# Batch 0's second half of x on ScalarE's queue, and its first two weight sums in chunks

## The chip, the cores and the metric

The kernel runs on one core of a Trainium2 chip. The metric is the time of one execution on the device, in microseconds (us); a comparison is made from the median of several executions. All data are 32-bit floats.

## What is computed

The reference takes x of shape (8, 256, 1024), a bank of eight 1024 x 1024 adapters, a base weight with bias, a router and a low-rank mixture of experts:

```python
w = weight[adapter_ids]                        # one 1024 x 1024 adapter per batch element
y = einsum('bsi,boi->bso', x, w)               # the "cond" product
base_out = einsum('btd,od->bto', y, base_W) + base_b
probs = softmax(einsum('btd,nd->btn', y, router_W) + router_b)
w = top-8 of the 15 probabilities, each given to its expert by expert_map
h = einsum('btd,erd->bter', y, A)
lora = einsum('bter,eor->bto', h * w[..., None], Bm) * 2.0
out = x + base_out + lora
```

Only the first line pair matters here: for each of the eight batch elements, x[b] (256 x 1024) is multiplied by its own adapter, which is read from memory (4 MB for each batch element).

## The kernel before

The kernel has two stages. In the first, a loop over the eight batch elements makes y by a Strassen-Winograd product: the adapter and x are cut into 2 x 2 quarters (`a11`, `a12`, `a22`, `a21` of the adapter, `b11`, `b12`, `b21`, `b22` of x), and seven products of quarters take the place of eight. In the second stage the base weight is multiplied in the same way, over pairs of batch groups. The change touches only what happens for batch element 0, in the first 30 us of the first stage.

A quarter of the adapter is a tile `wt` of 128 partitions x 4 chunks x 512 elements (1 MB); for batch 0 it is loaded in two halves of two chunks, 512 KB each, by `load_w` (line 366). The halves are called a11h0, a11h1 and so on here. x of batch 0 comes in two halves too, 512 KB each, by `load_x0` (line 372): half 0 holds b11 and b21, half 1 holds b12 and b22. Half 0 is issued on ScalarE's queue as the first thing; half 1 is issued on SyncE's queue (SP), between the two halves of a12. So SP's queue holds, in this order: a11h0, a11h1, a12h0, x half 1, a12h1, a22h0, a22h1, a21h0, a21h1, and then the loads of batch 1.

TensorE multiplies in the order that the code writes it down: first 13 matrix products of an identity (`idle`, nothing is read from them), then for batch 0 the blocks

1. a11 . b11 into `pa`, a12 . b21 into `pb` (need x half 0 alone)
2. a22 . T4 into a second `pb` (needs x half 1, since T4 comes from all quarters of x)
3. S1 . T1 into `pc`, S2 . T2 into `pa`
4. S4 . b22 into `pc`, S3 . (b22 - b12) into `pa`

A block is four chunk products (line 297). [...]

VectorE makes the sums, also in the order of the code: `turns` makes T1, T2, T4 and b22 - b12 from x (lines 399 to 404, four instructions of 128 x 512), then `first_sum` S1 = a21 + a22 (line 412, for batch 0 in two halves, one for each half of a21), `second_sum` S2 = S1 - a11 (line 416, one instruction of 128 x 2048), `fourth_sum` S4 = a12 - S2 (line 424), `third_sum` S3 = a11 - a21 (line 420).

All engines but GpSimd follow the order of the code in this stage (a manual schedule). The `wt` tiles share eight buffers; a load of batch 1 can be issued when the buffer it gets is free, and SP waits at it.

Of the kernel before, what the change touches and what calls it, by code (L numbers as in the profile page):

```python
# [10 lines left out]
F32 = mybir.dt.float32  # L11
# [17 lines left out]
def kernel(  # L29
# [16 lines left out]
    nc = tc.nc  # L46
    P = 128
# [3 lines left out]
    KH = 4  # L51
    OH = 512
# [11 lines left out]
    wpool = ctx.enter_context(tc.tile_pool(name="w", bufs=8))  # L64
# [32 lines left out]
    late = const.tile([P, 4 * OH + 2 * KC * S // 2 + 512], F32, name="late")  # L97
# [4 lines left out]
    def place(*shape):  # L102
# [18 lines left out]
        for name, shape in dict(  # L121
            h=[NTT, ER], lg=[NTT, N], mx=[NTT], ex=[NTT, N], den=[NTT], rden=[NTT],
# [148 lines left out]
    with ExitStack() as phase:  # L271
# [84 lines left out]
        def load(b):  # L356

            x = xpool.tile([P, 2, 2, KH, P], F32, name="x")
            q = {}

            def load_w(name, i, halves=None):
                if name not in q:
                    q[name] = wpool.tile([P, KH, OH], F32, name="wt")
                t = q[name].rearrange("p (h k) o -> p h (k o)", h=2)
                for h in [slice(0, 2)] if halves is None else [ts(n, 1) for n in halves]:
                    nc.sync.dma_start(
                        t[:, h],
                        wq[ds(adapter, 1), i, h].rearrange("e h p f -> p (e h) f"),
                    )

            def load_x0(j, engine):
                engine.dma_start(x[:, j].rearrange("p i k t -> p (i k t)"), x0[j])

            if b == 0:

                load_x0(0, nc.scalar)
            else:
                nc.sync.dma_start(x.rearrange("p j i k t -> p (j i k t)"), xq[b - 1])
            adapter = nc.sync.value_load(
                ids_sb[0:1, b : b + 1], min_val=0, max_val=NA - 1  # L380
            )
            if b == 0:
                load_w("a11", 0, (0, 1))
                load_w("a12", 1, (0,))
                load_x0(1, nc.sync)
                load_w("a12", 1, (1,))
                load_w("a22", 3, (0, 1))
                load_w("a21", 2, (0, 1))
            else:

                for name, i in (("a22", 3), ("a21", 2), ("a11", 0), ("a12", 1)):
                    load_w(name, i)
            return x, q

        def turns(x):

            b11, b12, b21, b22 = x[:, 0, 0], x[:, 1, 0], x[:, 0, 1], x[:, 1, 1]
            t1 = tpool.tile([P, KH * P], F32, name="tt").rearrange("p (k t) -> p k t", k=KH)
            nc.vector.tensor_sub(t1, b12, b11)
            t2 = tpool.tile([P, KH * P], F32, name="tt").rearrange("p (k t) -> p k t", k=KH)  # L400
            nc.vector.tensor_sub(t2, b22, t1)
            t4 = tpool.tile([P, KH * P], F32, name="tt").rearrange("p (k t) -> p k t", k=KH)
            nc.vector.tensor_sub(t4, b21, t2)
            nc.vector.tensor_sub(b12, b22, b12)
            return t1, t2, t4

        def first_sum(q):
            q["s1"] = wpool.tile([P, KH, OH], F32, name="wt")
            parts = 2 if q is first else 1
            for n in range(parts):  # L410
                h = ts(n, KH // parts)
                nc.vector.tensor_add(q["s1"][:, h], q["a21"][:, h], q["a22"][:, h])  # L412

        def second_sum(q):
            q["s2"] = wpool.tile([P, KH, OH], F32, name="wt")
            nc.vector.tensor_sub(q["s2"], q["s1"], q["a11"])

        def third_sum(q):

            nc.vector.tensor_sub(q["a21"], q["a11"], q["a21"])  # L420

        def fourth_sum(q):
            q["s4"] = wpool.tile([P, KH, OH], F32, name="wt")
            nc.vector.tensor_sub(q["s4"], q["a12"], q["s2"])

        phase.enter_context(
            tc.manual_schedule(engines={EN.PE, EN.DVE, EN.Activation, EN.SP})
        )
        x, q = load(0)
        first = q  # L430

        idle = ps.tile([P, OH], F32, name="pb")
        for _ in range(13):
            nc.tensor.matmul(idle[:, :P], lhsT=ident, rhs=ident, start=True, stop=True)
        t1, t2, t4 = turns(x)
        first_sum(q)
        second_sum(q)
        fourth_sum(q)
        third_sum(q)
        waiting = None  # L440
        behind = deque()
        for b in range(B):
# [3 lines left out]
            if not last:  # L446
                x, nq = load(b + 1)
# [51 lines left out]
            if b == 0:  # L499
                by_s4()  # L500
                by_s3()
                nc.vector.tensor_add(m1[:, 0], pa, m1[:, 0])
                flip(m1[:, 0], m1[:, 0])
                first_sum(nq)
                second_sum(nq)
                fourth_sum(nq)
            elif not last:
                first_sum(nq)
                by_s4()
                if b == 1:  # L510

                    by_s3()
                    second_sum(nq)
                else:
                    second_sum(nq)
                    by_s3()
# [24 lines left out]
            if not last:  # L541
                q, t1, t2, t4 = nq, nt1, nt2, nt4
# [470 lines left out]
```

## Time and profile before

| what | value |
|---|---|
| median of 3 runs | 429.84 us (429.76 to 430.26) |
| the profiled execution, its own time | 430.95 us |
| span of the profiled execution | 429.2 us |
| TensorE matrix products | 423.7 us busy, 99% of the span |
| VectorE | 338.0 us, 79% |
| ScalarE | 163.7 us, 38% |
| bytes moved by DMA | 93.15 MB, 217 GB/s on average |
| issue of x half 1 on SP | 0.43 us, from issue to landing 7.5 us |
| one S1 half (128 x 1024), S2, S4, S3 (128 x 2048) on VectorE | 1226, 2292, 2292, 2283 ns |

The span is the time from the first to the last instruction of the profiled execution; its own time is 1.75 us longer. In the profile PE is TensorE's matrix product, PEld its weight load, DVE is VectorE, ACT is ScalarE, SPq and ACTq are the instructions by which SP and ScalarE issue transfers. A row of the timeline gives the start, the busy time, the engine and line, output and input tiles, how many instructions were merged, and in brackets how long the engine had been idle and what released it.

### The profile page before, as it was taken

The numbers are of one execution on the slowest core, as the hardware profiler recorded it, in microseconds if no ns is written. First come the engines' busy times: TensorE is split into PE (matmuls) and PEld (weight loads), VectorE is DVE, ScalarE is ACT, GpSimd is POOL, SyncE is SP. The second block draws the span as 40 slices with busy tenths as digits, with TensorE's granted clock in tenths as the row PEclk, the third lists the DMA queues.
The fourth block names the chain that finished last, engine by engine and source line by source line (L and its number), as shares of the span: only waits on it lengthen the run. The fifth ranks groups of instructions, "written<-read, shape, count | busy, mean of one in ns | idle before, by whom it ended". The sixth has DMA issues, their size and how long they took to land.

```text
span 429.2 us, 4059 instructions
## 1 busy us (share of the span) xinstructions
PE 423.7 (99%) x1246; PEld 218.0 (51%) x1246; DVE 338.0 (79%) x520; ACT 163.7 (38%) x442; POOL 35.3 (8%) x57
## 2 busy tenths in 40 slices
PE   8999999999999999999999999999999999999997
PEld 5444464644645546446446565445454454544444
DVE  0699999986887898898995668889983499848783
ACT  1119367965667658666826722300000000211000
POOL 0000000000000000000003401203321050000000
PEclk9999999999999999999999999999999999999999
DMA  7997987869677789592595250027182201715935
GB/s 245 417 361 281 324 337 289 281 246 359 198 274 244 290 314 348 213 356 93 184 413 187 98 220 1 2 65 302 43 326 98 73 0 47 272 49 168 348 122 195
DMA packets 26408, 93.15 MB, mean 217 GB/s; under 512 B 2322, under 2 KB 6290, under 8 KB 24082
## 3 DMA queue, kind: packets, MB, share of 16 engines
q1 hardware_dynamic: 26242, 92.36, 58.7%
q10 hardware_dynamic: 144, 0.52, 0.3%
q8 instruction: 10, 0.16, 0.2%
q14 instruction: 12, 0.10, 0.1%
HBM read 71.65 MB, written 21.23 MB: 216 GB/s over the span
## 4 chain that ended last, share of the span: by engine, by line
PE 91%; DVE 4%; DMA 4%; SPq 1%; issue 0%; DVEq 0%
PE pa L297 24%; PE pa L581 20%; PE pc L297 13%; PE pc L581 10%; PE pb L297 7%; PE ph L135 6%; PE pb L684 4%; PE pc L590 2%; DMA wt<-in_wq_dram 2%; DMA out_dram<-q 1%; PE pa L590 1%; DVE q L794 1%; PE pb L688 1%; DVE late L793 1%; PE pa L135 1%; DVE q L783 1%
## 5 line engine op out<-in xcount | busy, mean ns | idle before, releaser
L315 ACT COPY y<-late 32x256 f32<-32x256 f32 x256 | 103.0, 402 | 42.0 <-DVE late L250 39.1
L581 PE MATMUL pa<-wt 128*128 128x512 f32 x168 | 76.2, 593 | 0.1
L297 PE MATMUL pa<-wt,x 128*128 128x512 f32 x128 | 57.6, 593 | 0.4 <-DMA wt<-in_wq_dram 0.4
L297 PE MATMUL pa<-wt,tt 128*128 128x512 f32 x120 | 54.0, 593 | 0.0
L581 PEld LDWEIGHTS pa<-wt 128*128 128x128 f32 x168 | 31.8, 190 | 35.7 <-issue 32.8
L636 ACT COPY q<-pa 128x512 f32<-128x512 f32 x6 | 3.5, 586 | 106.1 <-PE pa L581 91.3
L297 PEld LDWEIGHTS pa<-wt,x 128*128 128x128 f32 x128 | 24.2, 190 | 30.9 <-issue 29.7
L261 ACT COPY hwT<-late 32x64 f32<-32x64 f32 x128 | 31.1, 243 | 16.1 <-DVE late L250 14.6
L297 PEld LDWEIGHTS pa<-wt,tt 128*128 128x128 f32 x120 | 22.3, 190 | 26.2 <-issue 25.9
L135 PEld LDWEIGHTS ph<-late,y 128*128 128x128 f32 x224 | 28.4, 189 | 3.3 <-issue 3.3
L297 PE MATMUL pb<-wt,x 128*128 128x512 f32 x64 | 29.1, 595 | 0.6 <-DMA wt<-in_wq_dram 0.6
L297 PE MATMUL pc<-wt,x 128*128 128x512 f32 x64 | 28.9, 594 | 0.0
L297 PE MATMUL pc<-wt,tt 128*128 128x512 f32 x64 | 28.8, 592 | 0.0
L135 PE MATMUL ph<-late,y 128*128 128x143 f32 x224 | 28.6, 284 | 0.0
L581 PE MATMUL pa<-y,wt 128*128 128x512 f32 (+1 forms) x64 | 26.4, 552 | 0.0
L581 PE MATMUL pc<-y,wt 128*128 128x512 f32 x56 | 26.3, 592 | 0.0
L581 PE MATMUL pc<-wt 128*128 128x512 f32 x56 | 25.8, 592 | 0.0
L412 DVE TENSOR_TENSOR wt<-wt 128x2048 f32<-128x2048 f32 (+1 forms) x9 | 18.4, 2046 | 7.9 <-PE pa L297 5.5
L667 POOL TENSOR_TENSOR wt<-wt 128x128 f32<-128x128 f32 x6 | 3.1, 512 | 261.3 <-DVE spare L341 219.5
L250 DVE STREAM_TRANSPOSE late<-late 128x512 f32<-128x512 f32 (+1 forms) x33 | 21.4, 647 | 1.1
L297 PEld LDWEIGHTS pb<-wt,x 128*128 128x128 f32 x64 | 12.0, 190 | 16.6 <-issue 14.3
L297 PEld LDWEIGHTS pc<-wt,x 128*128 128x128 f32 x64 | 12.1, 190 | 15.5 <-issue 14.8
(131 smaller groups left out, 537.7 us busy)
## 6 DMA issues: line engine op xcount, KB each, us to landing
wt<-in_wq_dram SPq DMA_DIRECT2D x28, 1024.0 KB, 5.5
x<-in_xq_dram SPq DMA_DIRECT2D x7, 1024.0 KB, 7.0
wt<-left_raw SPq DMA_DIRECT2D x7, 1024.0 KB, 7.6
xt<-in_xr_dram SPq DMA_DIRECT2D x12, 512.0 KB, 5.6
wt<-left_sum SPq DMA_DIRECT2D x7, 768.0 KB, 8.9
wt<-in_wq_dram SPq DMA_DIRECT2D x8, 512.0 KB, 8.2
spare<-in_bq_dram SPq DMA_DIRECT2D x4, 1024.0 KB, 5.2
left_raw<-spare SPq DMA_DIRECT2D x4, 1024.0 KB, 6.3
```

Of the source, the lines that this page charges most:

```text
L135: nc.tensor.matmul(ph[:, j, : ER + N], lhsT=y[:, k // KH, k % KH // 2, th, k % 2, bi, ts(j, P)], rhs=ar_sb[:, k, :], start=(j == order[0] ...
L250: nc.vector.transpose(half, of)
L261: lambda a=a, r=r: nc.scalar.copy(to[32 * r : 32 * r + 32, :, a, :], hw[32 * a : 32 * a + 32, :, ts(r, 32)],)
L297: nc.tensor.matmul(acc, lhsT=right[:, k, :], rhs=left[:, k, :], start=(first and k == 0), stop=(k == KH - 1), skip_group_check=True,)
L315: lambda a=a, r=r: nc.scalar.copy(y[32 * r : 32 * r + 32, :, :, a, :], m[32 * a : 32 * a + 32, :, :, r, :])
L412: nc.vector.tensor_add(q["s1"][:, h], q["a21"][:, h], q["a22"][:, h])
L581: nc.tensor.matmul(acc, lhsT=left[:, 2 * k + mi, :], rhs=right[:, k, at], start=(first and k == 0), stop=(up is None and k == 1), skip_gro ...
L590: nc.tensor.matmul(acc, lhsT=up[:, ts(mi, P)], rhs=hw[:, at], start=False, stop=True, skip_group_check=True,)
L684: nc.tensor.matmul(acc, lhsT=d, rhs=e, start=first, stop=not joins, skip_group_check=True)
L688: nc.tensor.matmul(acc, lhsT=ups[n], rhs=hw[:, 0, h], start=False, stop=True, skip_group_check=True,)
L783: add(q, q, xs[oh, th, i, j])
L793: soon.append(lambda: add(v[:, i, j], v[:, i, j], q))
```

## The change

Three things are done, all for batch 0. First, x half 1 moves from SP's queue to ScalarE's. ScalarE first copies one column of a11's first half into a corner of `late`, so that the transfer is issued only once a11h0 has landed. Second, the two halves of a12 are then loaded one after the other on SP. Third, S1 and S2 are made chunk by chunk and in turns: S1 of chunks 0 and 1, S2 of chunks 0 and 1, S1 of chunks 2 and 3, S2 of chunks 2 and 3, in place of S1 in two halves and S2 whole. Later batch elements make S1 and S2 as they did.

```diff
             if b == 0:
                 load_w("a11", 0, (0, 1))
-                load_w("a12", 1, (0,))
-                load_x0(1, nc.sync)
-                load_w("a12", 1, (1,))
+
+                nc.scalar.copy(late[:, :1], q["a11"][:, 0, :1])
+                load_x0(1, nc.scalar)
+                load_w("a12", 1, (0, 1))
                 load_w("a22", 3, (0, 1))
                 load_w("a21", 2, (0, 1))
...
         def first_sum(q):
             q["s1"] = wpool.tile([P, KH, OH], F32, name="wt")
-            parts = 2 if q is first else 1
-            for n in range(parts):
-                h = ts(n, KH // parts)
-                nc.vector.tensor_add(q["s1"][:, h], q["a21"][:, h], q["a22"][:, h])
+            nc.vector.tensor_add(q["s1"], q["a21"], q["a22"])
...
+        def first_sums(q):
+
+            for name in ("s1", "s2"):
+                q[name] = wpool.tile([P, KH, OH], F32, name="wt")
+            for h in range(2):
+                for k in (2 * h, 2 * h + 1):
+                    nc.vector.tensor_add(q["s1"][:, k], q["a21"][:, k], q["a22"][:, k])
+                for k in (2 * h, 2 * h + 1):
+                    nc.vector.tensor_sub(q["s2"][:, k], q["s1"][:, k], q["a11"][:, k])
...
         x, q = load(0)
-        first = q
...
         t1, t2, t4 = turns(x)
-        first_sum(q)
-        second_sum(q)
+        first_sums(q)
         fourth_sum(q)
         third_sum(q)
```

## The prediction

> **What bounds the kernel now.** I read the page first, then the waits of TensorE, then the timeline and the windows of the first 30 us.
>
> ```profile
> span 429.2 us, 4059 instructions
> PE 423.7 (99%) x1246; PEld 218.0 (51%) x1246; DVE 338.0 (79%) x520; ACT 163.7 (38%) x442; POOL 35.3 (8%) x57
> PEclk9999999999999999999999999999999999999999
> ```
>
> TensorE is busy all but 5.5 us, at full granted clock. The waits of TensorE's products after 26 us are an empty list, and those before 30 us are these:
>
> ```profile
> PE pb L434 <- POOL ident masks.py:199: 1.4, 1, 1.4
> PE pb L297 <- DMA wt<-in_wq_dram: 0.6, 1, 0.6
> PE pa L297 <- DMA wt<-in_wq_dram: 0.4, 1, 0.4
> ```
>
> So a time saved or lost before TensorE's S4 block (25.65 us) moves the end by as much, and nothing later can give it back. How much there is to win stands in TensorE's own timeline:
>
> ```profile
> 6.44 1.88 PE L297 MATMUL pa<-wt,x 128*128 128x512 f32 x4
> 8.76 1.98 PE L297 MATMUL pa<-wt,x 128*128 128x512 f32 x4 [0.44 <-DMA wt<-in_wq_dram]
> 10.72 1.98 PE L297 MATMUL pb<-wt,x 128*128 128x512 f32 x4
> 13.29 1.98 PE L297 MATMUL pb<-wt,x 128*128 128x512 f32 x4 [0.59 <-DMA wt<-in_wq_dram]
> 15.12 3.60 PE L297 MATMUL pb<-wt,tt 128*128 128x512 f32 x8
> 18.55 3.60 PE L297 MATMUL pc<-wt,tt 128*128 128x512 f32 x8
> 22.14 3.67 PE L297 MATMUL pa<-wt,tt 128*128 128x512 f32 x8
> 25.65 3.60 PE L297 MATMUL pc<-wt,x 128*128 128x512 f32 x8
> 29.08 1.45 PE L297 MATMUL pa<-wt,x 128*128 128x512 f32 x3
> ```
>
> Eight rows back to back take 3.43 us (25.65 to 29.08), one row 0.429. From 6.44 to 25.65 are 40 rows, 17.15 us, in 19.21: 2.06 us are lost. Of these 1.71 go before 13.29, waiting for a11h1, a12h0 and a12h1 in turn, 0.12 for restarting at 13.29 (1.83 us for four rows), and 0.24 around S2 (3.59 and 3.51 where 3.43 would do).
>
> The transfers are what is waited for. In half-microsecond windows (last two columns: DMA share, GB/s):
>
> ```profile
> 6.50:7.00 0.50, 0.50 (x3) 0.26 (x3) 0.00 (x0) 0.00 (x0) 0.00 (x0) 1.00 0.62 238
> 7.00:7.50 0.50, 0.50 (x3) 0.25 (x2) 0.00 (x0) 0.00 (x0) 0.00 (x0) 1.00 2.12 164
> 7.50:8.00 0.50, 0.50 (x2) 0.00 (x0) 0.00 (x0) 0.00 (x0) 0.00 (x0) 1.00 0.35 139
> 8.00:8.50 0.50, 0.32 (x1) 0.00 (x0) 0.00 (x0) 0.00 (x0) 0.00 (x0) 1.00 0.50 205
> 12.00:12.50 0.50, 0.50 (x2) 0.00 (x0) 0.44 (x1) 0.00 (x0) 0.00 (x0) 1.00 0.98 401
> ```
>
> From 9 us on the engines move some 418 GB/s without a pause, so a half of 512 KB takes 1.25 us; between 6.5 and 8.5 they stall, with packets in flight (a share of 2.12) but few bytes. In the packet records a dozen engines sit for 0.5 to 1.6 us on one 4 KB packet that began at 7.06 to 7.33, as a12h0 begins. The last of the 16 engines' reports of each transfer, also in the trace, gives the landings: a11h0 6.17, a11h1 8.72, a12h0 10.67, x half 1 11.96, a12h1 13.25, a22h0 14.53, a22h1 15.80, a21h0 17.09, a21h1 18.35.
>
> **The change, part by part.**
>
> *x half 1 leaves SP's queue.* SP saves one issue (0.43 us, plus about 0.2 of steps between). That is worth nothing by itself: a12h1 was issued at 5.06 us and landed at 13.25, so the queue's backlog, not SP, sets the landings. The issues of a22h0 to a21h1 come 0.6 us earlier in the same backlog.
>
> *ScalarE waits for a11h0, copies, issues.* a11h0 is there at 6.17; the copy of one column is some 0.24 us by the nearest row (32x64 copies, 243 ns), the issue 0.38 (x half 0's row). Behind the wait on ScalarE stands only the copy of `pa` at 10.78, four us later: hidden, and if that cover went, m0's copy delays nothing before the add at 26.44. First bytes come about 1.1 us after the start of an issue (x half 0: issue 0.74, first packet 1.86), so at 7.5 us.
>
> *What the second queue does to the landings.* [...] The trace has no stretch with both queues busy. [...] By the row of the stall, instead, x half 1 could fill the idle half of 7.5 to 8.5 us: 279 and 213 GB/s missing, 246 KB, and everything later lands 0.59 us earlier. [...]
>
> [...] T4 becomes the bound only if x lands after 12.9.
>
> *S1 and S2 by chunks.* Removed: two instructions of 1226 ns and one of 2292. Added: eight of 128 x 512. In `turns` a chunk of this size lasts 0.69 us, and starts follow 0.61 apart where an instruction doesn't need the one before it (13.52 to 14.13), 0.73 where it does. Each S2 chunk needs the S1 chunk two places earlier, so 0.61 holds: the eight end 7 x 0.61 + 0.69 = 4.96 us after the first begins, against 21.99 - 17.11 = 4.88 before. [...]
>
> What TensorE gains: S2's first chunks are ready at about 19.6, long before 22.1, so the 0.24 goes. [...]
>
> *Buffers.* SP's order of waits shows one shift: batch 1's a12 gets another buffer, that of batch 0's a11, and waits for S3 (ends at about 26.6) where it had been issued at 24.9. Queued behind it are the load of `spare` and the constants, 1.7 us later. Cover: batch 1's a12 is first used at 35.9, the constants at 42.2, landing before that at about 35.7. No cost.
>
> **Sum.** Middle landing: 15.12, 18.55, 21.98, 25.41, so -0.24 us. Late landing: 15.35, 18.78, 22.21, 25.64, so -0.01. With the chunk rule's price +0.1 to +0.3 of that back. I take -0.15: the profiled execution's 430.95 becomes 430.8. The profiled time is 1.1 us above the median of the runs; the difference carries over, 429.84 - 0.15 = 429.7 us.
>
> **Rivals.**
>
> *The second queue fills the stall.* For it: the engines are idle, not short of work, from 7.5 to 8.5. Against it: the sitting packets may block the whole engine. Worth: a12h0 at 11.3, a12h1 at 12.7, a21h0 at 16.5, so a22 . T4 begins at 14.9 and S4 at 25.2: -0.5; if the stall from 7.0 on also eases, 373 KB or 0.89 us, -0.75; if a12's first packets no longer stall, up to -1.3. Near 429.0.
>
> *The second queue adds a stall (slower).* The first packets of several transfers sit for long: about 0.6 us for x half 1 itself on four engines, 1.3 us and more for a12h0 on a dozen. If x's first packets, now amid a12h0's, sit 1.3 us and hold up SP's packets too, all later landings move by 1.3: a12h0 at 13.0, a22 . T4 at 16.6, a21h0 at 18.4, S4 at 26.9: +1.2, 431.0. It decides from about 0.8 us of added stall on. Against it: bytes and addresses are the same.
>
> *It doesn't do what it says.* If x half 1 gets its place only behind SP's backlog, the order is much as before: between -0.24 and 0, as T4 has 0.9 us of slack.
>
> **How the numbers follow.** About 0.2% (0.86 us) is what a measurement of this kernel can tell from no change. The likeliest case has 0.52, of which 0.49 lie within 0.86 us, 0.02 faster and 0.01 slower; its own range is 429.4 to 430.1. Filling the stall has 0.24: 0.19 over the bound, 0.05 within. The added stall has 0.21: 0.20 over, 0.01 within. The last rival has 0.03, within. Sums: faster 0.21, same 0.58, slower 0.21. The range 428.8 to 430.9 leaves out 1 in 10 at each end.
>
> **What would show it.** Right: a12h0 lands later than 10.67 and x half 1 by 12; a21h0 near 17.1; S1's third chunk at about 20.2; no wait before S2; S4's first product between 25.4 and 25.65. Wrong: a21h0 off 17.1 by more than 0.6 us, x half 1 after 12.9, or a wait of TensorE after 26 us.

## The result and the profile after

The changed kernel takes 432.32 us in the median of 6 runs (431.47 to 433.63). The kernel before, run beside it, takes 430.02 (429.76 to 430.26, 6 runs). The ratio is 1.0054, with a 95% interval of 1.0042 to 1.0066: slower by 2.3 us. The forecast was no measurable change at 429.7 us, with a range up to 430.9; the result lies outside it.

The six runs fall into two groups by the granted clock (the share of TensorE's full clock that the records show as granted). Three have 1.0 over the whole span and take 431.47, 431.55 and 431.73 us. Three have 0.995 to 0.996 and take 432.91 to 433.63. All six runs of the kernel before have 0.999 or 1.0. So there are two losses to explain: some 1.5 us in every run, and another 1.6 us in some of them. The profiled execution is the one of 431.55 us. From its page:

```profile
span 429.8 us, 4065 instructions
PE 422.4 (98%) x1246; PEld 218.0 (51%) x1246; DVE 337.4 (78%) x525; ACT 163.9 (38%) x443; POOL 36.3 (8%) x57
```

TensorE is busy for 1.3 us less than before, and the span is longer by 0.6: the difference is idle time. The waits of TensorE's products name it in one line:

```profile
PE pb L297 <- DVE tt L404: 2.8, 1, 2.8
```

The waits of before for a11h1 and a12h1 (0.4 and 0.6 us) are gone. One wait of 2.8 us for T4 (`tt`, made at line 404 of this kernel) has taken their place. TensorE's timeline shows where it lies:

```profile
6.29 3.67 PE L297 MATMUL pa<-wt,x 128*128 128x512 f32 x8 [0.17 <-DMA wt<-in_wq_dram]
9.98 3.70 PE L297 MATMUL pb<-wt,x 128*128 128x512 f32 x8
16.45 3.67 PE L297 MATMUL pb<-wt,tt 128*128 128x512 f32 x8 [2.77 <-DVE tt L404]
19.96 3.60 PE L297 MATMUL pc<-wt,tt 128*128 128x512 f32 x8
23.39 3.60 PE L297 MATMUL pa<-wt,tt 128*128 128x512 f32 x8
26.83 3.60 PE L297 MATMUL pc<-wt,x 128*128 128x512 f32 x8
```

The blocks of a11 and a12 now run without a gap, and end some 1.5 us earlier than before. Then TensorE stands for 2.77 us, and a22 . T4 begins at 16.45 instead of 15.12. S4 begins at 26.83, 1.18 us later than before. ScalarE's and VectorE's timelines show both ends of the cause:

```profile
6.18 0.19 ACT L385 COPY late<-wt 128x1 f32<-128x1 f32 x1 [3.75 <-DMA wt<-in_wq_dram]
6.19 0.34 ACTq L372 DMA_DIRECT2D x<-in_x_dram  x1
```

```profile
14.21 0.69 DVE L400 TENSOR_TENSOR tt<-x 128x512 f32<-128x512 f32 x1 [14.21 <-DMA wt<-in_wq_dram]
14.94 0.69 DVE L402 TENSOR_TENSOR tt<-x,tt 128x512 f32<-128x512 f32 x1
15.66 0.69 DVE L404 TENSOR_TENSOR tt<-x,tt 128x512 f32<-128x512 f32 x1
```

The gate opened and the transfer was issued at 6.19 us, as forecast. But VectorE's first sum of x starts at 14.21, 2.15 us later than before. (The releaser printed, a transfer of `wt`, is the one that happened to come last; the sum reads x alone, and x half 1's last report is at 14.11.) The packet records of the transfers put numbers on it: first packet, and the last of the 16 reports.

| transfer | before, landed | after, landed |
|---|---|---|
| a12h0 | 10.67 | 9.94 |
| x half 1 | 11.96 | 14.11 (issued 6.19, first packet 9.95) |
| a12h1 | 13.25 | 11.23 |
| a22h0 | 14.53 | 13.48 |
| a21h0 | 17.09 | 16.36 |

x half 1's first packet moved 3.76 us after its issue, when a12h0 was already there. So a12h0 shared the engines with nothing, and x half 1 overlapped the end of a12h1 and then a22h0. Between 11.0 and 12.5 us it got about half (331 of the 620 KB in the packet records); over its whole 3.71 us (9.95 to 13.66) its 512 KB are 141 GB/s, a third of the 418 that the engines move together.

After S4's first product everything is as it was. From there to the last row of TensorE's timeline the changed kernel takes 399.55 us (26.83 to 426.38), and so do six of the profiles of the experiments below, within 0.01. The first profile of before takes 400.13 (25.65 to 425.78): 0.15 of the excess is a wait at batch 1's S4, and 0.43 is a stall at 412 us. These 0.58 are why the two profiled times differ by 0.60 (430.95 and 431.55) where S4 differs by 1.18. From that last row to the run's own time it is 5.17 us in both. So the profiles show 1.03 us of the 1.5 between the medians: S4's 1.18 less the 0.15. The rest goes with the profiled executions of before, which stand above their median (see "The kernel before again"); why they do stays open.

### The profile page after: what moved, and what is told of

It is laid out like the page before. It is cut to its first block, busy times and chain, and to the rows that moved or that the text cites. A ratio compares the mean times of both kernels' runs of the same rounds, so it can differ in the third digit from the quotient of the medians.

```text
span 429.8 us, 4065 instructions
## 1 busy us (share of the span) xinstructions
PE 422.4 (98%) x1246; PEld 218.0 (51%) x1246; DVE 337.4 (78%) x525; ACT 163.9 (38%) x443; POOL 36.3 (8%) x57
## 4 chain that ended last, share of the span: by engine, by line
PE 95%; DMA 2%; SPq 1%; DVE 1%; issue 0%
PE pa L297 24%; PE pa L587 23%; PE pc L297 13%; PE pc L587 11%; PE pb L297 6%; PE ph L135 6%; PE pb L690 4%; PE pc L596 3%; DMA wt<-in_wq_dram 2%; PE pa L596 2%; PE pb L694 1%; PE pa L135 1%; PE pb L587 1%; SPq L366 1%; PE pb L596 0%; DMA ids_sb<-in_ids_dram 0%
## 5 line engine op out<-in xcount | busy, mean ns | idle before, releaser
L410 DVE TENSOR_TENSOR wt<-wt 128x2048 f32<-128x2048 f32 x7 | 16.0, 2281 | 5.5 <-PE pa L297 5.5
L297 PEld LDWEIGHTS pc<-wt,tt 128*128 128x128 f32 x64 | 12.2, 190 | 15.3 <-issue 14.8
```

The source lines that it names most:

```text
L297: nc.tensor.matmul(acc, lhsT=right[:, k, :], rhs=left[:, k, :], start=(first and k == 0), stop=(k == KH - 1), skip_group_check=True,)
L410: nc.vector.tensor_add(q["s1"], q["a21"], q["a22"])
```

## The experiments

The theory from this profile was: what costs the time is that x half 1's packets start late, and they start late because of what is in SP's queue when it is issued. Its rivals were a fixed delay of some 3.5 us on ScalarE's second transfer, the changed order of a12 and x by itself, and the chunked sums.

### The chunked sums alone

The loads of before, with S1 and S2 in chunks:

```diff
-        first_sum(q)
-        second_sum(q)
+        first_sums(q)
```

> The kernel before with S1 and S2 of batch 0 made chunk by chunk, x half 1 left where it was on SP's queue. Theory (the loss of the change comes from the queue alone, the chunks remove the S2 wait): S4's first product at 25.4 us in place of 25.65, time 0.2 us under the kernel before (429.8). Rival (the eight small sums cost: S1's third chunk comes late): a wait of 0.3 us or more within S1 x T1, time equal to or 0.1 to 0.3 us over before.

Measured: 430.04 us (13 runs) against 430.02, ratio 1.0000 (0.9992 to 1.0009). The chunks are not what made the kernel slower. The gain expected of them is not there either. TensorE's timeline and the waits of its weight loads say why:

```profile
17.44 3.71 PE L297 MATMUL pc<-wt,tt 128*128 128x512 f32 x8
20.99 3.60 PE L297 MATMUL pa<-wt,tt 128*128 128x512 f32 x8
24.42 3.60 PE L297 MATMUL pc<-wt,x 128*128 128x512 f32 x8
48.75 1.45 PE L297 MATMUL pa<-wt,x 128*128 128x512 f32 x3
```

```profile
PEld pc L297 <- DVE wt L421: 1.2, 3, 0.7
PEld pc L297 <- ACT late L499: 0.9, 1, 0.9
```

S2 follows S1 directly, and S4 follows S2 after 3.43 us, so the loss around S2 is gone. But S1 . T1 takes 3.55 us, since S1's third chunk is late (the first line of the waits, 0.7 at most). Of 0.24 us half is left, and the second line takes that back at batch 1's S4. From S4's first product to batch 1's S3 it is 24.33 us (24.42 to 48.75), where the changed kernel, without this wait, takes 24.03.

### The same chunks, all of S1 first

```diff
-            for h in range(2):
-                for k in (2 * h, 2 * h + 1):
+            for k in range(KH):
                     nc.vector.tensor_add(q["s1"][:, k], q["a21"][:, k], q["a22"][:, k])
-                for k in (2 * h, 2 * h + 1):
+            for k in range(KH):
                     nc.vector.tensor_sub(q["s2"][:, k], q["s1"][:, k], q["a11"][:, k])
```

> The kernel before with S1 in four chunks and then S2 in four chunks (all of S1 first, not in turns). Theory (with the chunks in turns the gain at S2 is lost again at S1's third chunk, which stood behind two S2 chunks): no wait of TensorE in S1 x T1 other than for a21h1, none before S2; S4's first product 0.3 to 0.6 us before that of the chunks in turns for like landings, time 0.2 to 0.5 us under the kernel before. Rival (the landings set the end, whatever the order of the sums): no difference over 0.15 us.

Measured: 430.33 (13 runs) against 430.20, ratio 1.0002 (0.9993 to 1.0010). In its profile S1 . T1 has no gap (18.07 to 21.50, 3.43 us) and S4 begins at 24.93, 0.5 later than with the chunks in turns, since a21h0 landed 0.63 later (16.62 and 15.99). But batch 1's S4 then waits 1.1 us for `late` (ScalarE's copy of `pc`), and from S4 to batch 1's S3 it is 24.57 us. The earlier S4 was handed back a batch later, as in the kernel with the chunks alone.

### The gate on x half 0

The transfer is issued at 4.16 us instead of 6.19:

```diff
-                nc.scalar.copy(late[:, :1], q["a11"][:, 0, :1])
+                nc.scalar.copy(late[:, :1], x[:, 0, 0, 0, :1])
```

> The changed kernel, but ScalarE's copy waits for x half 0 (lands at about 4.0 us) in place of a11h0 (6.17), so that x half 1 is issued at about 4.1 us, when SP has issued three transfers and not seven. Theory (a transfer of the second queue starts only behind what SP had issued long before: the delay is backlog): the first packet of x half 1 comes 1 to 2 us after its issue, at 5 to 6 us, not 3.7 us after it; it lands by 10, T4 is no bound, TensorE's wait of 2.8 us is gone, S4's first product at 25.0 to 25.6 us, time 429.4 to 430.0. Rival (an issue behind a wait on ScalarE always takes some 3.7 us to its first packet, or the second queue is served last): first packet at 7.8 us or after, landing at about 11.5 to 12; TensorE's wait shrinks to under 0.5 us as well, but the first packet tells the two apart.

Measured: 430.50 (13 runs) against 430.02, ratio 1.0012 (1.0004 to 1.0020); most of the loss is gone. The first packet came at 7.51, which is 3.35 us after the issue: nearly as late after it as in the changed kernel (3.76), so the 5 to 6 us expected were missed, and this run alone fits a fixed delay as well. Here x half 1 does share with a12, and the forecast's late landing happened almost to the digit (a12h0 at 11.73; the late case supposes 11.75, an estimate between 10.67 and 11.96, where a12h0 and x half 1 landed before, so in part by luck):

```profile
11.78 3.70 PE L297 MATMUL pb<-wt,x 128*128 128x512 f32 x8 [0.99 <-DMA wt<-in_wq_dram]
15.31 3.60 PE L297 MATMUL pb<-wt,tt 128*128 128x512 f32 x8
18.75 3.60 PE L297 MATMUL pc<-wt,tt 128*128 128x512 f32 x8
22.18 3.60 PE L297 MATMUL pa<-wt,tt 128*128 128x512 f32 x8
25.61 3.60 PE L297 MATMUL pc<-wt,x 128*128 128x512 f32 x8
```

The prediction's late landing has 15.35, 18.78, 22.21 and 25.64 for first bytes at 7.5 us: a12's block from 11.8 on (11.78 here), then 3.43 us for its eight rows and 0.12 for restarting. With that input its late case was right; it was the input that was wrong.

### SP held before a22

To shorten what is queued, SP waits until a11h0 is there (it stores 4 bytes of it to a scratch in memory) before it issues a22:

```diff
                 load_w("a12", 1, (0, 1))
+                nc.sync.dma_start(hold, q["a11"][:1, 0, :1])
                 load_w("a22", 3, (0, 1))
```

> The changed kernel, but SP waits for a11h0 (by a 4-byte store of one of its elements to a scratch in memory) before it issues a22h0, so that SP has four transfers issued when x half 1 is issued at 6.2 us, and not seven. The gate of x half 1 is unchanged. Theory (backlog): first packet of x half 1 at 7.3 to 8.5 us in place of 9.9, landing by 11.5 to 12.3, TensorE's wait for T4 under 0.5 us, S4's first product at 25.2 to 25.8, time 429.6 to 430.3. Rival (an issue behind a wait on ScalarE takes 3.7 us by itself): first packet still at 9.9, landing at 12.5 or after, wait for T4 over 1 us, time 431 or more.

Measured: 431.44 (6 runs) against 430.02, ratio 1.0037 (1.0023 to 1.0051). First packet at 9.60, 3.33 us after the issue at 6.27; x half 1 there at 13.88. The expectation of 7.3 to 8.5 was missed. (Two of the six runs, 432.89 and 433.12 us, have a clock of 0.995 and 0.996. The second of them is the profiled one; the clock is taken up below, and all the times here lie before it drops, at 16.71.) Leaving a22 and a21 out of the queue changes little; if the queue is the cause, it is what stands directly ahead: a11h1, then under way, and a12h0.

### SP held before a12

The same store one line earlier, so that only a11h1 is left in SP's queue when x half 1 is issued:

```diff
+                nc.sync.dma_start(hold, q["a11"][:1, 0, :1])
                 load_w("a12", 1, (0, 1))
```

> The changed kernel, but SP waits for a11h0 already before a12h0 (by a 4-byte store of one of its elements to a scratch in memory), so that when ScalarE issues x half 1 at 6.2 us only a11h1 is under way in SP's queue. Theory A (a transfer of the second queue waits for what stands in the DMA engines at its issue: in three profiles its first packet came as the transfer in progress and the next one had ended): first packet at 7.2 to 7.9 us, 1.0 to 1.6 after the issue; x half 1 and a12h0 share the engines and land at 9.5 to 11; no wait for T4; time 429.8 to 430.8. Theory B (an issue on ScalarE behind a wait takes 3.3 to 3.9 us to its first packet whatever the queue holds): first packet at 9.5 to 10, landing at 11.5 or later.

This is the run that decides. From ScalarE's, SP's, VectorE's and TensorE's timelines:

```profile
6.17 0.34 ACTq L374 DMA_DIRECT2D x<-in_x_dram  x1
```

```profile
6.63 3.55 SPq L368 DMA_DIRECT2D wt<-in_wq_dram  x6
```

```profile
9.97 0.69 DVE L403 TENSOR_TENSOR tt<-x 128x512 f32<-128x512 f32 x1 [9.97 <-DMA x<-in_x_dram]
```

```profile
11.18 3.70 PE L299 MATMUL pb<-wt,x 128*128 128x512 f32 x8 [1.24 <-DMA wt<-in_wq_dram]
14.72 3.60 PE L299 MATMUL pb<-wt,tt 128*128 128x512 f32 x8
```

Issued at the same time as in the changed kernel, the first packet came at 7.15, after 0.98 us, and x half 1 was there at 9.87 instead of 14.11. The fixed delay falls. Measured: 430.66 (18 runs) against 430.20, ratio 1.0013 (1.0006 to 1.0020). Now a12h0 is the one that is late (11.14), and TensorE waits 1.24 us for it; that is the price of holding the main queue, and the 2.3 us are not there.

The packet records of this run answer one more rival, that ScalarE's queue is served only after SP's. a12h0 was issued on SP at 6.63 us, 0.46 after x half 1, while a11h1 was under way. Its first packet moved at 8.91, 2.28 us after the issue, as x half 1's packets ran out (the last ended at 9.51; SP's store of 4 bytes stood ahead of it too). From 7.2 to 8.9 only ScalarE's queue moved bytes. So the delay belongs to neither queue: here it is SP's transfer that starts behind ScalarE's, where the expectation had the two sharing.

The first packets on ScalarE's queue, side by side:

| kernel | issue | first packet | later by | ahead in SP's queue |
|---|---|---|---|---|
| x half 0 (changed kernel) | 0.74 | 1.77 | 1.03 | nothing |
| SP held before a12 | 6.17 | 7.15 | 0.98 | a11h1 |
| gate on x half 0 | 4.16 | 7.51 | 3.35 | a11h0, a11h1 and more |
| SP held before a22 | 6.27 | 9.60 | 3.33 | a11h1, a12 |
| changed kernel | 6.19 | 9.95 | 3.76 | a11h1, a12, a22, a21 |

In each of the last three rows the packets begin as the second of SP's transfers ends: a11h1 (7.21 to 8.37 across the engines) in the first of them, a12h0 (8.67 to 10.23) in the second. In the second profile of the changed kernel and in the one with half of the fill (both below) it is 0.4 and 0.6 us after a12h0's last report. So in these runs a transfer on one queue started behind the one that was under way and the next that was issued before it, 512 KB each. Whether these are held in the DMA engines or in what hands transfers to them isn't settled by these runs.

### x half 1 on SP, last

The order of a12 and x alone, without a second queue (the chunked sums stay):

```diff
-                nc.scalar.copy(late[:, :1], q["a11"][:, 0, :1])
-                load_x0(1, nc.scalar)
                 load_w("a12", 1, (0, 1))
+                load_x0(1, nc.sync)
```

> The changed kernel with x half 1 issued on SP's queue directly behind a12h1, and no copy on ScalarE: the new order of landings without the second queue. Theory (the loss is x half 1 landing late at 14.1, of which the place behind a12 is a part and the start of the second queue 3.7 us after its issue is the rest): it lands at 12.2 to 13.3, T4 ends 2.3 later, TensorE waits 0.5 to 1.8 us for it, S4's first product at 25.2 to 26.2 us, time 430.2 to 431.3, between before and after, with few or no runs at a lower mean clock. Rival (the order alone costs nothing, it is the second queue): time within 0.3 of before.

Measured: 430.18 (12 runs) against 430.20, ratio 1.0001 (0.9992 to 1.0009). In TensorE's timeline:

```profile
15.26 3.67 PE L297 MATMUL pb<-wt,tt 128*128 128x512 f32 x8 [1.14 <-DVE tt L402]
25.64 3.60 PE L297 MATMUL pc<-wt,x 128*128 128x512 f32 x8
```

x half 1 lands at 12.92, which is the 12.9 from which the prediction let T4 become the bound, and the block begins 0.14 later than before. The expectation, that the order is part of the loss, was missed, and its rival holds: the order alone costs nothing. The loss is the rest, 12.92 to 14.11.

### Filling TensorE's wait

So the late landing of x half 1 is the cause of the part that every run has. For the other part, the clock, TensorE's wait is filled with products of the identity from which nothing is read, first 12, then 6:

```diff
                 pd = ps.tile([P, OH], F32, name="pb")
+                for _ in range(12):
+                    nc.tensor.matmul(pd[:, :P], lhsT=ident, rhs=ident, start=True, stop=True)
                 block(pd, q["a22"], t4, True)
```

> The changed kernel with 12 products of the identity (128 columns, nothing is read from them) ahead of a22 x T4, which fill TensorE's wait of 2.8 us for T4. Theory (the runs of the changed kernel at 433 us, with a mean clock of 0.995, lose some 1.5 us since the clock gate lowers the clock for a window after the idle time): all runs at clock 1.0 and at 431.4 to 431.7, median 431.5. Rival (the spread comes from the transfers): the runs spread from 431.5 to 433.6 as before, median over 432.

Measured: 431.90 (5 runs) against 430.02, ratio 1.0044 (1.0031 to 1.0057), all at a clock of 0.999 or 1.0. The fill was too long: in the profiled execution, the slowest (432.63), it ended only at 17.6 us and delayed the block itself. So it doesn't separate the clock's cost from its own. The changed kernel was run again for more executions, and with half of the fill:

> The changed kernel once more, beside the next one. Theory (the clock gate drops the clock for one window of 3.4 us when the wait for T4 falls within one of its windows): the runs stand in two groups, about 431.6 at mean clock 0.999 to 1.0 and about 433 at 0.995 to 0.996, a third to two thirds of them in the second. Rival (the second group was chance in the first six runs): one group, all at clock 1.0.

> The changed kernel with 6 products of the identity (1.3 us of TensorE at full clock, nothing is read from them) ahead of a22 x T4, which end before T4 is there and so delay nothing; about half of the wait of 2.8 us stays idle. Theory (the clock drops since a window of 3.4 us is idle for most of it): no run at a mean clock under 0.998, all in one group at 431.2 to 431.9. Rival (the groups are unrelated to the idle time): two groups, 431.6 and 433, as in the changed kernel.

The changed kernel again: 433.25 (5 runs) against 430.10, ratio 1.0078 (1.0051 to 1.0104). One run has a clock of 0.999 (431.84), three have 0.996 (433.11 to 433.38), one 0.991 (435.58). This time the profiled execution is one of the lower clock. Its windows, cut where the clock's records change (16.65 and 20.07) and 3.41 us apart; the columns are the window, its length, busy time of PE, PEld, DVE, ACT and POOL, the granted clock, DMA share and GB/s:

```profile
13.24:16.65 3.41, 0.90 (x3) 0.30 (x2) 2.52 (x4) 0.00 (x0) 0.00 (x0) 1.00 1.04 424
16.65:20.07 3.42, 3.42 (x5) 1.33 (x4) 3.42 (x7) 0.00 (x0) 0.00 (x0) 0.50 1.01 418
20.07:23.48 3.41, 3.41 (x9) 1.52 (x8) 3.38 (x4) 0.59 (x1) 0.00 (x0) 1.00 0.66 226
```

In the window before the change TensorE is busy for 0.90 us; the next one runs at half of the clock, the one after at full clock again. TensorE's timeline shows what that costs:

```profile
16.30 5.37 PE L297 MATMUL pb<-wt,tt 128*128 128x512 f32 x8 [2.51 <-DVE tt L404]
21.51 3.60 PE L297 MATMUL pc<-wt,tt 128*128 128x512 f32 x8
```

The block takes 5.21 us from start to start (16.30 to 21.51), and 3.51 in the first profile (16.45 to 19.96); the difference, 1.70, is half of the 3.42 us at half clock. The wait itself is shorter than in the first profile (2.51 and 2.77), where the clock stayed at 1.0. There the clock had risen at 4.74 us, and windows of 3.41 us counted from that moment cut the idle time in two:

```profile
11.56:14.98 3.42, 2.12 (x5) 0.58 (x4) 0.74 (x2) 0.00 (x0) 0.00 (x0) 1.00 1.03 417
14.98:18.39 3.41, 1.94 (x5) 1.01 (x6) 3.38 (x6) 0.00 (x0) 0.00 (x0) 1.00 1.05 435
```

Neither window is mostly idle. The run with SP held before a22 is a second case of the drop. Its records change at 16.71 and 20.12, and the wait of 2.25 us lies inside the window ahead of that:

```profile
13.30:16.71 3.41, 1.16 (x3) 0.30 (x2) 2.66 (x5) 0.00 (x0) 0.00 (x0) 1.00 1.03 421
16.71:20.12 3.41, 3.41 (x5) 1.33 (x4) 3.41 (x7) 0.00 (x0) 0.00 (x0) 0.50 1.01 418
```

In these four windows the clock was halved after 0.90 and 1.16 us of work and kept after 1.94 and 2.12; what comes of a window between these no run shows. The half clock lasts 3.42 and 3.41 us in the two profiles, the stretch of full clock ahead of it 10.24, three times as long, and the clock's rise falls anywhere from 4.30 to 7.29 us in the profiles here. Where the clock stays, no record marks a window: that windows of 3.41 us follow one another from the rise on is the author's reading of these lengths. Each of the waits of 2.51 and 2.25 us lay inside one window, and the next was halved.

With 6 products in the wait, 4 of 4 runs are at 1.0: 431.80 (431.20 to 432.10) against 430.10, ratio 1.0042 (1.0026 to 1.0057), and TensorE's timeline has

```profile
13.26 1.50 PE L496 MATMUL pb<-ident 128*128 128x128 f32 x12
16.03 3.70 PE L297 MATMUL pb<-wt,tt 128*128 128x512 f32 x8 [1.27 <-DVE tt L404]
```

Two of the four lie a little over the 431.9 expected. Without a fill 4 of 11 runs kept the clock, with one 9 of 9 did. Four runs are few, but 433 to 435 us does not occur among the nine. The run of 435.58 and 0.991 has no profile; by its clock (0.996 in the two profiles with one halved window) it lost more than one, an estimate.

### The kernel before again

> The kernel before, once more with a profile. Theory (the profiled execution of before that the forecast used had a longer stall of the transfers at 7 us than is usual, and so stands 0.9 us over the median): a21h0 lands nearer to 16 than to 17.1, S4's first product at 24.5 to 25.1 us in place of 25.65, time about 430.0. Rival (the difference is not in the first 26 us): S4's first product at 25.65 and another time all the same.

One more profile, nothing changed: 430.63 us, S4 at 25.74, a21h0 at 17.18. From S4 to the last row it takes 399.69, so the stall at 412 us of the first profile was that execution's own, and the 0.15 at batch 1 is the kernel's. The landings, though, are again as late as in the first profile, and the theory that those were unusual is not borne out. By S4 plus 399.69 plus 5.17, the median of 430.02 would have S4 at 25.2 (an estimate; no profile of before shows it). Why both profiled executions of before are above its median stays open.

### A version that beats both

What the runs leave is: keep x half 1 on SP, last, and shorten the 1.14 us wait for T4 that this order has. T1, T2 and T4 of batch 0 are made in two halves, so that the first half of T4 is there sooner, and all of S1 before S2:

```diff
-        def turns(x):
+        def turns(x, parts=1):
...
+            for n in range(parts):
+                h = ts(n, KH // parts)
+                nc.vector.tensor_sub(t1[:, h], b12[:, h], b11[:, h])
+                nc.vector.tensor_sub(t2[:, h], b22[:, h], t1[:, h])
+                nc.vector.tensor_sub(t4[:, h], b21[:, h], t2[:, h])
```

> The kernel before with x half 1 behind a12h1 on SP's queue, the T1, T2, T4 of batch 0 made in two halves (chunks 0 and 1, then 2 and 3), and S1 in four chunks, then S2 in four. Theory (TensorE is bound by the later of a12 and the first half of T4, and by a21h0): T4's first half is ready 1.35 us after x half 1, which lands at about 12.9, so a22 x T4 begins at 14.2 to 14.4 in place of 15.1 to 15.3, S4's first product at 24.6 to 24.9, time 0.3 to 1 us under the kernel before. Rival (a later part of the kernel takes the gain back, or a21h0 sets the start of S1 x T1 anyway): S4's first product at 25 or later, or early without effect on the time: within 0.2 us of before.

Measured: 430.42 (11 runs) against 430.10, ratio 1.0009 (1.0000 to 1.0018): no gain. TensorE's, ScalarE's and VectorE's timelines:

```profile
14.15 3.67 PE L297 MATMUL pb<-wt,tt 128*128 128x512 f32 x8 [0.32 <-DVE tt L405]
24.53 3.60 PE L297 MATMUL pc<-wt,x 128*128 128x512 f32 x8
45.82 3.70 PE L297 MATMUL pc<-wt,x 128*128 128x512 f32 x8 [0.53 <-ACT late L500]
```

```profile
31.40 8.29 ACT L315 COPY y<-late 32x256 f32<-32x256 f32 x20 [6.09 <-DVE late L250]
40.19 4.95 ACT L315 COPY y<-late 32x256 f32<-32x256 f32 x12
45.18 0.59 ACT L500 COPY late<-pc 128x512 f32<-128x512 f32 x1
```

```profile
29.34 0.69 DVE L406 TENSOR_TENSOR x<-x 128x512 f32<-128x512 f32 x1
29.94 0.68 DVE L481 TENSOR_TENSOR late<-pc,late 128x512 f32<-128x512 f32 x1
30.66 0.71 DVE L250 STREAM_TRANSPOSE late<-late 128x512 f32<-128x512 f32 x1
```

S4 begins 1.1 us earlier than before, and batch 1's S4 waits for it to come back. The wait is for a copy on ScalarE, which stands behind 32 moves, which wait for a transpose on VectorE, which waits for the add of S4's result at 29.94. S4's block is done by 28.1, but the add stands behind batch 1's four T sums, the last of which begins at 29.34. This second chain sets when batch 1's S4 can begin, however early batch 0's S4 was. So the four T sums are put behind the add:

```diff
-            if not last:
+            if not last and b > 0:
                 nt1, nt2, nt4 = turns(x)
...
                 by_s4()
+                nt1, nt2, nt4 = turns(x)
                 by_s3()
```

> The version with x half 1 last, T4 in halves and all of S1 first, and beside that VectorE makes batch 1's T1, T2, T4 after the sum and transpose of batch 0's S4 block (line 481 of it) and not ahead of them. Theory (what that version had won by S4 was taken back at batch 1's S4 block, where TensorE waited 1.4 us for ScalarE's copy of pc, which stood behind ScalarE's 20 moves of batch 0's results, which waited for VectorE's transpose at 30.7 us, itself behind batch 1's T sums): the transpose ends about 1.8 us earlier, the wait at batch 1's S4 block is gone (0.24 or less), time 0.6 to 1.2 us under the kernel before, 428.9 to 429.6. Rival (another wait takes its place, on the loads of batch 1 or at the end): the wait for the copy is gone but another of 0.5 us or more stands later; time within 0.3 us of before.

Measured: 429.27 us (429.06 to 430.15, 11 runs) against 429.95 (15 runs), ratio 0.9985 (0.9976 to 0.9994). That beats both kernels, by 0.7 us and, from ratio to ratio, by some 3. The chain's links moved, and the wait is gone (VectorE's transpose, ScalarE's copy, TensorE's two S4 blocks):

```profile
28.93 0.71 DVE L250 STREAM_TRANSPOSE late<-late 128x512 f32<-128x512 f32 x1
```

```profile
43.45 0.58 ACT L500 COPY late<-pc 128x512 f32<-128x512 f32 x1
```

```profile
24.50 3.60 PE L297 MATMUL pc<-wt,x 128*128 128x512 f32 x8
45.10 3.60 PE L297 MATMUL pc<-wt,x 128*128 128x512 f32 x8
```

From S4 to batch 1's S3 it is 24.04 us (24.50 to 48.54), as in the kernels without the wait; it was 24.82 in the version ahead of it.

## Why the prediction was wrong, step by step

**First bytes of x half 1 at 7.5 us: this step failed.** It took the 1.1 us from issue to first packet from x half 0's row, which was issued into empty queues. With SP's queue filled it was 3.76 us. Had the step been 9.95, the working would have put x half 1 behind a12h0 and beside a22h0. Its landing would have been between 12.9 and 14.5 (estimates: at half of 418 GB/s its 512 KB take 2.5 us, and the last report came 0.45 after the last packet; at the late end, all bytes that share are in by a22h0's 14.53). It was 14.11. T4 is the bound from 12.9 on (before, its sums took 2.15 us, 12.06 to 14.21, and the block began at 15.12), so the block would begin up to 1.6 us late. It was 1.33 late, and S4 1.18. That a12h0 and x half 1 share the engines from 8 us on, as the middle and late landings suppose, was the author's assumption: here a12h0 had landed at 9.94 before x half 1's first packet moved at 9.95, and in the run with SP held before a12 only ScalarE's queue moved bytes from 7.2 to 8.9 us. That a21h0 lands as before is not contradicted: it came 0.7 earlier, not later (16.36), but its landing differs by 1.2 between profiles that have the order of before (15.99 to 17.18).

**What would show it.** Two of the prediction's three signs of being wrong came: x half 1 after 12.9, and a21h0 off 17.1 by more than 0.6. The second says little, given that spread.

**SP's saved issue is worth nothing, the gate opens at 6.17, the copy is hidden: right.** Issue at 6.19; ScalarE's next copy, of `pa`, followed at 10.06 without delay.

**a12h0 late, the block at 15.12 to 15.35: did not happen in this kernel,** since nothing shared with a12h0. No run shows the sum's middle landing (a22 . T4 at 15.12, S4 at 25.41): here they began at 16.45 and 26.83. The late landing came in the kernel gated on x half 0 alone, and that sum came out within 0.04 us at each block.

**The chunks' -0.24: half right.** The loss around S2 went. With the chunks alone S1's third chunk, forecast at about 20.2 and wanted at 20.26 (four rows of 0.429 after 18.55), was late and took 0.12 back (S1 . T1 in 3.55 us for 3.43); in the changed kernel, where T4 is late, it had time to spare (19.96 to 23.39). No run shows the price on small chunks, +0.1 to +0.3, that the sum uses: the eight took 4.90 us in the changed kernel (16.87 to 21.77) and 4.91 with the chunks alone (16.01 to 20.92), the three instructions of before 4.88 (17.11 to 21.99).

**The buffer's shift: right.** `spare`'s load was issued at 26.85 instead of 25.34, and no wait of TensorE came of it.

**Nothing later can give it back: wrong.** The prediction read this from an empty list of waits after 26 us. That list is of the products. Before, the weight loads' own list had the lines

```profile
PEld pa L581 <- DVE u L610: 1.6, 2, 0.9
PEld pc L297 <- ACT late L494: 0.7, 1, 0.7
```

and the products' pace shows that they cost some: 0.15 us around the second, which the later S4 of the changed kernel wins back, and which grows as S4 gets earlier (0.30 with the chunks alone, 0.79 in the version with T4 in halves, before batch 1's T sums were moved). It is also why gains of 0.1 to 1.1 us ahead of S4 didn't reach the end until the second chain was shortened.

**The granted clock: not in the prediction at all.** None of its cases asked what an idle TensorE does to the clock. It cost some 1.6 us more in 6 of the 11 runs of the changed kernel, and 3.7 to 4 in a seventh.

**The rivals.** The added stall named the right side and nearly the right numbers (431.0, S4 at 26.9), by another mechanism: it had packets of a12 sit and hold up all that follows, and a22 and a21 in fact came earlier. The filled stall did not show: x half 1 moved no byte in 7.5 to 8.5 us. "It doesn't do what it says" was nearest in mechanism, as x half 1 did get its place only behind part of SP's queue; but the prediction priced it as if the order of before were kept, with 0.9 us of slack for T4. That slack was counted from x's landing at 11.96; a landing 2.15 later used it up more than twice over. The packets that sat 1.3 us and more for a12h0, on which the added stall is priced, were eight in the records and not a dozen; nothing in the outcome hangs on it.

## What to carry to other kernels

Here a transfer on a second queue was not ahead of the first queue's backlog (3.76 us from issue to first packet, 0.98 with the backlog held): read its delay from a transfer that was issued while the other queue was full, or issue it before that queue fills. When one wait is removed, follow each consumer of what arrives later, and ask how long TensorE stands in one piece; here waits of 2.25 and 2.51 us cost some 1.7 us more each. And before a gain is carried to the end, read the weight loads' waits too, and the chain through the other engines that meets TensorE one batch later.

## What was not expected of the hardware

Transfers on two queues did not share the engines from the start. A transfer on ScalarE's queue began 3.3 to 4.1 us after its issue with two or more 512 KB transfers ahead in SP's queue (six profiles), and 1.0 to 1.1 us with one or none. One on SP's queue began 2.28 us after its issue, with a11h1 and ScalarE's x half 1 ahead of it. The clock went to half for one window of 3.41 us after windows in which TensorE had been busy for 0.90 and 1.16 us (gaps of 2.51 and 2.25); a gap of 2.77 us that fell across two windows, busy for 2.12 and 1.94, left it alone.
